# A graph-attention kernel: one node tile counted from ScalarE's steps, and T1 of head 0 summed on VectorE

## The chip, the core and the metric

The kernel runs on one core of a Trainium2 chip. The metric is the time of one execution on the device in microseconds (us), the median of a few runs. TensorE, VectorE (DVE), ScalarE (ACT), GpSimd (POOL) and SyncE (SP) each work through a queue of their own in order; semaphores connect them.

## What is computed

A two-layer graph attention network over 512 nodes with 768 features, a residual and a layer norm. There are 16,384 random edges, 8,192 in either direction, and 512 loops, 16,896 in all, sorted by destination. Per head of a layer:

```
h = x @ W                                    # 512 x 768
e = leaky_relu(h.a_s[src] + h.a_d[dst])
alpha = softmax of e over the edges of each dst
out[dst] = sum over its edges of alpha * h[src]   (+ b)
```

Layer 1 has 8 heads; its output (512 x 6144) goes through elu, and layer 2 has one head. The output is layernorm(x + layer 2).

## The kernel before

The edges enter only as counts. `cnt[dst, src]` says how many edges run from src to dst, and the softmax over edges becomes a dense softmax over 512 sources weighted by `cnt`; where there is no edge, `absent` holds a large number that pushes the exponent to zero. All matrix products of layer 1 are float32 and use a scheme with 7 products instead of 8 for each 2 x 2 block product (P1 to P7), so each head needs sums of blocks of its weights and of x: T1 = B11 + B12, T2 = T1 + B22, T3 = B12 + B22, T4 = T2 + B21 on the side of the weights, and `xS` with s1, s2, s4 (and s3 in place, in `xT`) on the side of x. P5 multiplies s1 by T1, P6 multiplies s2 by T2, P7 uses T3, P4 uses T4.

The start of the kernel, some 77 us, does three things at once. It loads x and the weights of heads 0 and 1. It counts the edges. And it projects head 0 (`first_projection`, 14 products) and the first four products of head 1. The order of all engines is written out by hand (`manual_schedule`).

**Counting.** The edges lie in 132 chunks of 128. For each chunk, `od` is a one-hot of the destination within a block of 32 nodes (the chunks are sorted, so a chunk touches one or two of the 16 blocks), and `os` is a one-hot of the source over 512 nodes. A matmul of `od` and `os` (L526) adds the chunk to 32 rows of a count in PSUM; four blocks of 32 rows make a node tile of 128, and four node tiles make the whole. 210 such matmuls are needed. `destinations` (L479) makes the `od` of a quarter of the chunks, `sources` the `os` of a batch of about 16 chunks: VectorE by one `is_equal` (L509), and from the third batch on a quarter of the chunks by ScalarE with two activations, |n - idx| and then relu(1 - that) (L502, L503). There are 32 `os` buffers. `count` sends the matmuls, and when a node tile is complete, `counted` copies it to `cnt` and makes `absent` (L393, L394). A program variable `flag` tells whether every edge fell within its chunk's blocks; if not, the whole is run again in a general way (it isn't here).

**The interleaving.** A loop over nine batches does, for each batch: the `od` of the quarters it needs, its `os`, some extra VectorE work (`extra`: the sums s1, s2, s4, s3, the logits of head 0), some products (`wants` says up to which one), and its counting matmuls. After the last products the logits are turned (`spread`, L434), lifted by ScalarE (L440), made leaky (L444) and ranked (L449) by VectorE. Then the remaining ten products of head 1 run beside the softmax of head 0.

**The weights of head 0.** W1[0] lies in `w0` (upper half) and `w1` (lower half); T1 lies in `w1t1`. SP loads `w0`'s and `w1`'s left halves, x, then the left half of the upper block into T1 (L150), then the right halves (L152), then the starts of T2 and T4 (L159). POOL then issues accumulating DMAs, each waiting for its operands, in this order: T1 += right half of the upper block (L378), T3 in place in `w0` (L379), T2 += T1 (L162), T4 += T2 (L163). The same loads and sums for head 1 follow on both queues (L105 to L117, L159 to L163).

Of the kernel before, what the change touches and what calls it, by code (L numbers as in the profile page):

```python
# [8 lines left out]
F32 = mybir.dt.float32  # L9
F16 = mybir.dt.float16  # L10
BF16 = mybir.dt.bfloat16
I32 = mybir.dt.int32
U16 = mybir.dt.uint16
AF = mybir.ActivationFunctionType
ALU = mybir.AluOpType
# [5 lines left out]
NO_EDGE = -1e30  # L21
# [15 lines left out]
def gat_pass(  # L37
# [16 lines left out]
    nc = tc.nc  # L54
# [66 lines left out]
    def load_w1(h, slot="w2"):  # L121
        return load_w(W1, h, slot, w1[:, h * D:(h + 1) * D])
# [15 lines left out]
    def block(m, r, cols):  # L138
        return m[r * HK * P:(r + 1) * HK * P, cols].rearrange("(k p) d -> p k d", p=P)
# [7 lines left out]
    b1_rows = ohp.tile([H * DC, P], F32, name="b1_rows")  # L147
    nc.sync.dma_start(b1_rows, b1.rearrange("(j p) -> j p", p=P))
    W1[0].append(wpool.tile([P, HK, HALF], F32, name="w1t1"))
    nc.sync.dma_start(W1[0][2], block(w1_0, 0, L))  # L150
    for r in (1, 0):
        nc.sync.dma_start(W1[0][r][:, :, R], block(w1_0, r, R))  # L152

    def sums_by_dma(W_, m, slot):

        lo_, hi_, t1_ = W_
        t2, t4 = (wpool.tile([P, HK, HALF], F32, name=f"{slot}t{j}") for j in (2, 4))
        for t_, cols in ((t2, R), (t4, L)):
            nc.sync.dma_start(t_, block(m, 1, cols))  # L159

        def additions():
            nc.gpsimd.dma_start(t2, t1_, accum_op=ALU.add)  # L162
            nc.gpsimd.dma_start(t4, t2, accum_op=ALU.add)  # L163
        return dict(P1=lo_[:, :, L], P2=hi_[:, :, L], P3=hi_[:, :, R], P4=t4, P5=t1_, P6=t2,
                    P7=lo_[:, :, R]), additions

# [152 lines left out]
    def logits(h, feats, t):  # L319
        for al, a, sign in zip(AL[h], A[h], (1.0, -1.0)):  # L320
            nc.vector.scalar_tensor_tensor(scr, feats[:, t, :], sign, a, op0=ALU.mult,
                                           op1=ALU.mult, accum_out=al[:, t:t + 1])
# [52 lines left out]
        ]  # L375
        return [pair(p, i, *rest) for p, *rest in steps for i in range(2)]

    nc.gpsimd.dma_start(W1[0][2], block(w1_0, 0, R), accum_op=ALU.add)  # L378
    nc.gpsimd.dma_start(W1[0][0][:, :, R], block(w1_0, 1, R), accum_op=ALU.add)  # L379
    additions0()  # L380

    load_w1(1, "w2")()
    B1, additions1 = sums_by_dma(W1[1], w1[:, D:2 * D], "w2")
    additions1()


    b1T = const.tile([P, H * DC], F32, name="b1T")
# [3 lines left out]
    def counted(t, ps):  # L391

        nc.scalar.copy(cnt[:, t, :], ps[:, :N])  # L393
        nc.scalar.activation(absent[:, t, :], ps[:, :N], AF.Relu, bias=far, scale=NO_EDGE)  # L394

    def first_projection(h, XA, B_):

# [64 lines left out]
    again = None  # L462
    if not general:

        order = []
        for g in range(NT):
            rs = [[c for c in range(EC) if int((c + 0.5) * P * N / E) // B == b] for b in range(g * 4, g * 4 + 4)]
            while any(rs):
                order.append([r.pop(0) for r in rs if r])
        hits = {}  # L470
        for b in (b for bs in blocks for b in bs):
            hits[b] = hits.get(b, 0) + 1
        todo = dict(hits)
        cps, done = {}, 0
        od = ohp.tile([P, NB, B], BF16, name="odw", bufs=1)

        def destinations(lo, hi):
            lo, hi = at[lo], at[hi]
            nc.vector.tensor_tensor(od[:, lo:hi, :],  # L479
                                    rel[:, lo:hi].unsqueeze(2).to_broadcast([P, hi - lo, B]),  # L480
                                    nodes[:, :B].unsqueeze(1).to_broadcast([P, hi - lo, B]),
                                    op=ALU.is_equal)

        def inside():
# [2 lines left out]
            nc.vector.tensor_scalar(below, rel, float(B), None, op0=ALU.is_lt)  # L487
            nc.vector.scalar_tensor_tensor(below, rel, 0.0, below, op0=ALU.is_ge, op1=ALU.mult, accum_out=found)


        nidx = ohp.tile([P, EC], F32, name="nidx")
        nc.scalar.activation(nidx, idx, AF.Copy, scale=-1.0)

        def sources(chunks, with_scalar, between):

            hot = {}
            shared = chunks[3::4] if with_scalar else []
            own = [c for c in chunks if c not in shared]
            for c in shared:
                hot[c] = ohp.tile([P, N], BF16, name="os", bufs=32)  # L500
                off = ohp.tile([P, N], F16, name="off", bufs=2)
                nc.scalar.activation(off, nodes, AF.Abs, bias=nidx[:, c:c + 1])  # L502
                nc.scalar.activation(hot[c], off, AF.Relu, bias=ones, scale=-1.0)  # L503
            for j, c in enumerate(own):
                if j == len(own) // 2:
                    for f in between:
                        f()
                hot[c] = ohp.tile([P, N], BF16, name="os", bufs=32)
                nc.vector.tensor_scalar(hot[c], nodes, idx[:, c:c + 1], None, op0=ALU.is_equal)  # L509
            return hot  # L510

        queues = [[] for _ in range(0, P, B)]

        def count(batch, hot, rest):


            nonlocal done
            for c, b in ((c, b) for wave in batch for c in wave for b in blocks[c]):
                queues[b * B % P // B].append((c, b, hot[c]))
            while any(queues) and (rest or all(queues) or sum(map(len, queues)) > 3):  # L520
                for c, b, h_ in [q_.pop(0) for q_ in queues if q_]:
                    t, r = b * B // P, b * B % P
                    if t not in cps:
                        pool, name = (bc, "bc") if t == 2 else (tr, "tr")
                        cps[t] = pool.tile([P, 512], F32, name=name)
                    nc.tensor.matmul(cps[t][r:r + B, :N], od[:, at[c] + b - blocks[c][0], :], h_,  # L526
                                     start=todo[b] == hits[b], stop=todo[b] == 1,
                                     tile_position=(0, r), skip_group_check=True)
                    todo[b] -= 1
            while done < NT and all(todo[b] == 0 for b in range(done * P // B, (done + 1) * P // B)):  # L530
                counted(done, cps[done])
                done += 1


        turns = {1: [(0, 1), (1, 1)], 3: [(2, 0), (3, 0), (2, 1), (3, 1)]}
        keep_warm(1)
        found = const.tile([P, 1], F32, name="found")
        pst = bc.tile([P, 512], F32, name="bc")
        wholes = len(items)

        s1, s2, s3, s4 = xsums
        extra = {0: [inside], 1: [s1, s2, s4], 3: [s3], 5: [lambda: logits(0, HS[0], 0)],
                 6: [lambda: logits(0, HS[0], 1), lambda: logits(0, HS[0], 2)], 7: [lambda: logits(0, HS[0], 3)]}
        wants = [3, 4, 7, 10, 12, 14, 16, 18]
        BW = 4
        batches = [order[i:i + BW] for i in range(0, len(order), BW)]
        pos, ready, quarter, waiting = 0, 0, EC // NT, []
        for n, batch in enumerate(batches):
            chunks = [c for wave in batch for c in wave]
            while ready <= max(chunks):  # L550
                destinations(ready, ready + quarter)
                ready += quarter
            if n == 3:
                nc.vector.tensor_scalar(flag, pst[:1, :1], -1.0, float(E), op0=ALU.mult, op1=ALU.add)
            hot = sources(chunks, n > 1, waiting)
            waiting = []
            for f in extra.pop(n, []):
                f()
            while n < len(wants) and pos < wants[n]:
                if pos == wholes:  # L560
                    pairs = projection(1, XA, B1)
                    items += [(m, e, False) for m, e in pairs[:4]]
                multiply, empty, on_vector = items[pos]
                multiply()
                if on_vector:
                    waiting.append(empty)
                else:
                    empty()
                pos += 1
                for t, r in turns.get(pos, []):  # L570
                    turn_x(t, r)
            if n == 2:
                turn_b1()
            if n + 1 == len(batches):
                spread(0)
                q = [lift(0, t) for t in range(NT)]
                for t in range(NT - 1):
                    leak(q[t])
                for t in range(NT - 1):
                    rank(q[t], t)  # L580
            if n == 1:
                nc.tensor.matmul(pst[:1, :1], found, ones, start=True, stop=True)
            if n == 4:
                again = nc.values_load(flag[:1, :1], min_val=0, max_val=E)
            count(batch, hot, n + 1 == len(batches))
        assert not extra and not waiting and pos == len(items) and done == NT
    else:
        for t in range(NT):
            ps = mm.tile([P, 512], F32, name="mm")
# [8 lines left out]
            for r in range(2):  # L598
                turn_x(t, r)
        turn_b1()  # L600
        for f in xsums:
            f()
        for m, e, _ in items:
# [441 lines left out]
```

## Time and profile before

| | us |
|---|---|
| median of 3 runs | 664.24 |
| lowest and highest | 663.87, 664.38 |
| the profiled execution | 663.6 |
| its span, first to last instruction | 661.8 |

| engine | busy us | share |
|---|---|---|
| TensorE matmuls | 645.7 | 98% |
| TensorE weight loads (beside them) | 400.1 | 60% |
| VectorE | 506.8 | 77% |
| ScalarE | 281.4 | 43% |
| GpSimd | 47.9 | 7% |

The profile describes one execution. "L306" is line 306 of the kernel; lines of the changed kernel differ. A row of a timeline gives the start, the length, the engine, the line, the operation with output<-input, shapes and a count, and in brackets how long the engine had been idle before and what released it. Waits are inferred from semaphore events, and some matmul records can be missing. TensorE has a granted clock, 1.00 for full and 0.50 for half; the profile lists it by stretches of time.

### The profile page before, as it was taken

To read this page: it belongs to the slowest core of one execution; us is meant where nothing else is said; L and a number is where in the kernel's file an instruction comes from. 1 tells how busy PE (TensorE), PEld (TensorE's weight loads), DVE (VectorE), ACT (ScalarE), POOL (GpSimd) and SP (SyncE) were. 2 spreads that over 40 slices of the span, in tenths; PEclk is the share of its full clock that TensorE was granted. 3 is DMA by queue.
4 is the path that set the end of the run, shared out by engine and by line. 5 is a ranking of instruction groups with operands and counts; after the bars stand their busy time and mean duration, and the time that the engine had idled before them with its cause. 6 is when DMAs were issued, how large, how long until landed. Compare 5 with 4: busy or idle time off the path is not lost.

```text
span 661.8 us, 7074 instructions
## 1 busy us (share of the span) xinstructions
PE 645.7 (98%) x2347; PEld 400.1 (60%) x2347; DVE 506.8 (77%) x1103; ACT 281.4 (43%) x477; POOL 47.9 (7%) x91
## 2 busy tenths in 40 slices
PE   9799899999999999999999999999999999999995
PEld 5354467555865577556855577556855545644553
DVE  7959689977778587777779587867676489866785
ACT  4289657260445216350635135440726033333440
POOL 3020011000100110010100110010000100000000
PEclk9799799999999999999999999999999999999998
DMA  9993179267902973077803892096605865000122
GB/s 321 289 272 89 35 241 279 76 167 164 269 14 49 265 209 90 14 222 162 215 0 75 239 241 58 17 255 195 146 1 146 217 213 132 24 1 0 30 59 76
DMA packets 74986, 92.06 MB, mean 139 GB/s; under 512 B 36742, under 2 KB 59326, under 8 KB 74942
## 3 DMA queue, kind: packets, MB, share of 16 engines
q1 hardware_dynamic: 60878, 69.31, 33.2%
q0 software_dynamic: 13376, 21.24, 18.6%
q10 hardware_dynamic: 688, 0.98, 0.5%
q8 instruction: 20, 0.33, 0.2%
q14 instruction: 24, 0.20, 0.1%
HBM read 79.20 MB, written 1.57 MB: 122 GB/s over the span
## 4 chain that ended last, share of the span: by engine, by line
PE 92%; DMA 4%; ACT 2%; issue 0%; DVE 0%; SPq 0%; ACTq 0%
PE mm L306 62%; PE mm L731 17%; PE mm L677 6%; DMA w1t<-in_L_gnn_W_dram 3%; PE mm L997 3%; PE held L306 2%; ACT off L502 1%; ACT os L503 1%; PE tr L526 1%; DMA hs<-in_x_dram 1%; PE bc L434 0%; PE tr L925 0%; PE tr L646 0%; PE bc L526 0%; ACT absent L394 0%
## 5 line engine op out<-in xcount | busy, mean ns | idle before, releaser
L306 PE MATMUL mm<-w,gT 128*128 128x384 f32 x288 | 97.4, 487 | 0.0
L306 PE MATMUL mm<-w,xT 128*128 128x384 f32 x264 | 88.2, 487 | 0.0
L306 PEld LDWEIGHTS mm<-w,gT 128*128 128x128 f32 x288 | 53.9, 190 | 35.7 <-issue 2.0
L306 PEld LDWEIGHTS mm<-w,xT 128*128 128x128 f32 x264 | 49.9, 190 | 35.5 <-issue 0.4
L451 ACT ACTIVATE q<-q,nmax 128x512 f32<-128x512 f32 x36 | 25.8, 721 | 89.9 <-DVE nmax L449 89.9
L306 PE MATMUL mm<-w1t,gS 128*128 128x384 f32 x180 | 60.7, 486 | 0.0
L306 PE MATMUL mm<-w2t,xS 128*128 128x384 f32 x168 | 58.2, 497 | 0.0
L735 ACT COPY u<-mm 128x256 f32<-128x256 f32 x18 | 6.7, 373 | 119.2 <-PE mm L731 119.2
L731 PE MATMUL mm<-PT,hs 128*128 128x256 f32 x216 | 52.6, 379 | 0.0
L364 DVE TENSOR_TENSOR h<-h,mm 128x384 f32<-128x384 f32 x72 | 39.6, 551 | 14.3 <-PE mm L306 13.8
L306 PEld LDWEIGHTS mm<-w1t,gS 128*128 128x128 f32 x180 | 34.1, 190 | 23.6
L306 PEld LDWEIGHTS mm<-w2t,xS 128*128 128x128 f32 x168 | 32.6, 195 | 23.6 <-issue 2.3
L731 PEld LDWEIGHTS mm<-PT,hs 128*128 128x128 f32 x216 | 41.0, 190 | 7.2 <-issue 0.4
L654 ACT COPY nr<-q 128x1024 uint16<-128x1024 uint16 x32 | 33.4, 1044 | 24.3 <-DVE q L640 17.5
L677 PE MATMUL mm<-PT,hs 128*128 128x512 f32 x96 | 41.6, 593 | 0.0
L659 ACT COPY PT<-zr 128x1024 uint16<-128x1024 uint16 x32 | 37.1, 1158 | 2.0 <-DMA zr<-nr 2.0
L731 PE MATMUL mm<-pS,gS 128*128 128x256 f32 x144 | 37.1, 380 | 0.0
L306 PE MATMUL mm<-w,gS 128*128 128x384 f32 x96 | 32.6, 486 | 0.0
L306 PE MATMUL mm<-w1t,gT 128*128 128x384 f32 x96 | 32.5, 487 | 0.0
L306 PE MATMUL mm<-w,xS 128*128 128x384 f32 x96 | 32.5, 487 | 0.0
L677 PEld LDWEIGHTS mm<-PT,hs 128*128 128x128 f32 x96 | 18.2, 190 | 22.9 <-issue 21.5
L106 POOL DMA_DIRECT2D w1t<-in_L_gnn_W_dram x7 | 9.0, 1279 | 316.7 <-PE mm L306 179.9
(183 smaller groups left out, 1079.8 us busy)
## 6 DMA issues: line engine op xcount, KB each, us to landing
w<-in_L_gnn_W_dram SPq DMA_DIRECT2D x90, 384.0 KB, 6.1
w<-in_L_gnn_W_dram POOLq DMA_DIRECT2D x16, 576.0 KB, 9.0
w1t<-in_L_gnn_W_dram SPq DMA_DIRECT2D x10, 576.0 KB, 4.5
w2t<-in_L_gnn_W_dram SPq DMA_DIRECT2D x10, 576.0 KB, 11.1
w1t<-in_L_gnn_W_dram POOLq DMA_DIRECT2D x8, 576.0 KB, 8.7
w2t<-in_L_gnn_W_dram POOLq DMA_DIRECT2D x8, 576.0 KB, 9.4
a_s<-in_L_gnn_a_src_dram SPq DMA_DIRECT2D x8, 384.0 KB, 5.1
a_d<-in_L_gnn_a_dst_dram SPq DMA_DIRECT2D x8, 384.0 KB, 5.4
```

What stands on the lines that cost most here:

```text
L106: nc.gpsimd.dma_start(t1, upper[:, :, R], accum_op=ALU.add)
L306: nc.tensor.matmul(ps[:, :HALF], A_[p][:, k, i * P:(i + 1) * P], B_[p][:, k, :], start=start and k == 0, stop=k == HK - 1, skip_group_chec ...
L364: nc.vector.tensor_tensor(a, a, ps, op=ALU.subtract if p == "P7" else ALU.add)
L451: nc.scalar.activation(q, q, AF.Exp, bias=nmax, scale=-1.0)
L502: nc.scalar.activation(off, nodes, AF.Abs, bias=nidx[:, c:c + 1])
L503: nc.scalar.activation(hot[c], off, AF.Relu, bias=ones, scale=-1.0)
L654: nc.scalar.copy(apart.rearrange("p (h n) -> p h n", h=2), q.bitcast(U16).rearrange("p (n h) -> p h n", h=2))
L659: nc.scalar.copy(PT.rearrange("p s n -> p (s n)").bitcast(U16).rearrange("p (s n h) -> p s n h", s=NT, h=2)[:, :, t * P:(t + 1) * P, :], p ...
L677: nc.tensor.matmul(ps[:, :N], HS[h][:, s, c * P:(c + 1) * P], PT[:, s, :], start=(s == 0), stop=(s == NT - 1))
L731: nc.tensor.matmul(bank[p][:, :HN], A_[p][:, k, c * P:(c + 1) * P], B_[p][:, k, :], start=over is None and k == 0, stop=k == 1, skip_group ...
L735: nc.scalar.copy(u, part("P1"))
L997: nc.tensor.matmul(ps[:, :cols.stop - cols.start], PT[:, s, t * P:(t + 1) * P], h2[:, s, cols], start=(s == 2), stop=(s == 1))
```

## The change

It has two parts, and what goes with them.

T1 of head 0 is no longer loaded and accumulated by DMA. VectorE adds the two halves of `w0` (128 x 1152 float32), and for that the right half of `w0` is loaded ahead of that of `w1`. The sums of the weights of both heads are now asked for inside the loop, in batch 1, in the order T1 (VectorE), T2, T3, T4.

The chunks of node tile S = 2 are taken out of the order of the others and spread over all batches. Their sources are made by ScalarE in one activation, as a step instead of a one-hot: sign(n + 0.5 - idx) is -1 below the source and 1 from it on. Half the difference of neighbouring columns of the summed steps is the count. `counted_by_steps` takes it from PSUM with a column put in front, VectorE takes the difference, and `absent` is made from that. All other chunks are VectorE's. A chunk that touches tile 2 and another tile is made in both forms. The steps of a batch are made a batch ahead, between the products. The sum for `flag` moves to another PSUM bank, and is made and read earlier.

```diff
     W1[0].append(wpool.tile([P, HK, HALF], F32, name="w1t1"))
-    nc.sync.dma_start(W1[0][2], block(w1_0, 0, L))
-    for r in (1, 0):
+    for r in (0, 1):
         nc.sync.dma_start(W1[0][r][:, :, R], block(w1_0, r, R))
...
-        def additions():
-            nc.gpsimd.dma_start(t2, t1_, accum_op=ALU.add)
-            nc.gpsimd.dma_start(t4, t2, accum_op=ALU.add)
+        additions = [lambda: nc.gpsimd.dma_start(t2, t1_, accum_op=ALU.add),
+                     lambda: nc.gpsimd.dma_start(t4, t2, accum_op=ALU.add)]
...
-    nc.gpsimd.dma_start(W1[0][2], block(w1_0, 0, R), accum_op=ALU.add)
-    nc.gpsimd.dma_start(W1[0][0][:, :, R], block(w1_0, 1, R), accum_op=ALU.add)
-    additions0()
-
-    load_w1(1, "w2")()
-    B1, additions1 = sums_by_dma(W1[1], w1[:, D:2 * D], "w2")
-    additions1()
+    def weight_sums():
+
+        nc.vector.tensor_tensor(W1[0][2], W1[0][0][:, :, L], W1[0][0][:, :, R], op=ALU.add)
+        additions0[0]()
+        nc.gpsimd.dma_start(W1[0][0][:, :, R], block(w1_0, 1, R), accum_op=ALU.add)
+        additions0[1]()
+        load_w1(1, "w2")()
+        B_, additions1 = sums_by_dma(W1[1], w1[:, D:2 * D], "w2")
+        for f in additions1:
+            f()
+        return B_
...
+    def counted_by_steps(t, ps):
+
+
+        steps = ohp.tile([P, N + 1], F32, name="steps")
+        nc.scalar.activation(steps[:, 1:], ps[:, :N], AF.Copy, scale=0.5)
+        nc.scalar.activation(steps[:, :1], ps[:, N - 1:N], AF.Copy, scale=-0.5)
+        nc.vector.tensor_tensor(cnt[:, t, :], steps[:, 1:], steps[:, :N], op=ALU.subtract)
+        nc.scalar.activation(absent[:, t, :], cnt[:, t, :], AF.Relu, bias=far, scale=NO_EDGE)
...
+        S = 2
+        order = {False: [], True: []}
...
-        nc.scalar.activation(nidx, idx, AF.Copy, scale=-1.0)
...
+        nc.scalar.activation(nidx, idx, AF.Copy, bias=0.5, scale=-1.0)
...
+        def one_hot(c, steps):
+            hot[c, steps] = o = ohp.tile([P, N], BF16, name="os", bufs=32)
+            if steps:
+                nc.scalar.activation(o, nodes, AF.Sign, bias=nidx[:, c:c + 1])
+            else:
+                nc.vector.tensor_scalar(o, nodes, idx[:, c:c + 1], None, op0=ALU.is_equal)
...
-        pst = bc.tile([P, 512], F32, name="bc")
...
-        extra = {0: [inside], 1: [s1, s2, s4], 3: [s3], 5: [lambda: logits(0, HS[0], 0)],
+        def ask():
+            nc.vector.tensor_scalar(flag, pst[:1, :1], -1.0, float(E), op0=ALU.mult, op1=ALU.add)
+
+        extra = {0: [inside], 1: [lambda: B1.update(weight_sums()), ask, s1, s2, s4], 3: [s3],
+                 5: [lambda: logits(0, HS[0], 0)],
...
-        BW = 4
-        batches = [order[i:i + BW] for i in range(0, len(order), BW)]
+        batches = []
+        for ours, theirs in ((16, 0), (8, 8), (8, 8), (12, 4), (12, 4), (12, 4), (13, 3), (14, 2), (4, 0)):
+            take = [order[k][:m] for k, m in ((False, ours), (True, theirs))]
+            del order[False][:ours], order[True][:theirs]
+            batches.append(take[0][:ours // 2] + take[1] + take[0][ours // 2:])
...
+            for k in sorted({c // quarter for c in batch} - made):
+                destinations(k * quarter, (k + 1) * quarter)
+                made.add(k)
+            sources(kinds(batch, False), waiting)
+            ahead = kinds(batches[n + 1], True) if n + 1 < len(batches) else []
+            items_here = max(wants[n] - pos if n < len(wants) else 0, 1)
+            share = -(-len(ahead) // items_here)
...
+                for c in ahead[:share]:
+                    one_hot(c, True)
+                del ahead[:share]
...
-            if n == 1:
+            if n == 0:
+                pst = mm.tile([P, 512], F32, name="mm")
                 nc.tensor.matmul(pst[:1, :1], found, ones, start=True, stop=True)
-            if n == 4:
+            if n == 3:
                 again = nc.values_load(flag[:1, :1], min_val=0, max_val=E)
```

More of the change, by code (lines that the diff above doesn't have):

```diff
@@ L463, in gat_pass @@
     if not general:
-        order = []
+        S = 2
+        order = {False: [], True: []}
         for g in range(NT):
@@ L468, in gat_pass @@
             while any(rs):
-                order.append([r.pop(0) for r in rs if r])
+                order[g == S] += [r.pop(0) for r in rs if r]
         hits = {}
@@ L473, in gat_pass @@
         todo = dict(hits)
-        cps, done = {}, 0
+        cps, done = {}, set()
         od = ohp.tile([P, NB, B], BF16, name="odw", bufs=1)
@@ L491, in gat_pass, with by_steps, kinds, sources @@
         nidx = ohp.tile([P, EC], F32, name="nidx")
-        nc.scalar.activation(nidx, idx, AF.Copy, scale=-1.0)
[L494 to L505, printed above, removed]
+        nc.scalar.activation(nidx, idx, AF.Copy, bias=0.5, scale=-1.0)
+        def by_steps(b):
+            return b * B // P == S
+        hot = {}
+        def one_hot(c, steps):
[4 more added lines that the diff above has]
+                nc.vector.tensor_scalar(o, nodes, idx[:, c:c + 1], None, op0=ALU.is_equal)
+        def kinds(batch, steps):
+            return [c for c in batch if any(by_steps(b) == steps for b in blocks[c])]
+        def sources(chunks, between):
+            for j, c in enumerate(chunks):
+                if j == len(chunks) // 2:
                     for f in between:
                         f()
-                hot[c] = ohp.tile([P, N], BF16, name="os", bufs=32)
-                nc.vector.tensor_scalar(hot[c], nodes, idx[:, c:c + 1], None, op0=ALU.is_equal)
-            return hot
+                one_hot(c, False)
         queues = [[] for _ in range(0, P, B)]
[L514 to L519, printed above, removed]
+        def count(batch, rest):
+            for c, b in ((c, b) for c in batch for b in blocks[c]):
+                queues[b * B % P // B].append((c, b, hot[c, by_steps(b)]))
             while any(queues) and (rest or all(queues) or sum(map(len, queues)) > 3):
@@ L523, in count @@
                     if t not in cps:
-                        pool, name = (bc, "bc") if t == 2 else (tr, "tr")
+                        pool, name = (bc, "bc") if t == S else (tr, "tr")
                         cps[t] = pool.tile([P, 512], F32, name=name)
@@ L529, in count @@
                     todo[b] -= 1
-            while done < NT and all(todo[b] == 0 for b in range(done * P // B, (done + 1) * P // B)):
-                counted(done, cps[done])
-                done += 1
+            for t in range(NT):
+                if t not in done and all(todo[b] == 0 for b in range(t * P // B, (t + 1) * P // B)):
+                    (counted_by_steps if t == S else counted)(t, cps[t])
+                    done.add(t)
         turns = {1: [(0, 1), (1, 1)], 3: [(2, 0), (3, 0), (2, 1), (3, 1)]}
@@ L537, in gat_pass @@
         found = const.tile([P, 1], F32, name="found")
-        pst = bc.tile([P, 512], F32, name="bc")
         wholes = len(items)
         s1, s2, s3, s4 = xsums
-        extra = {0: [inside], 1: [s1, s2, s4], 3: [s3], 5: [lambda: logits(0, HS[0], 0)],
+        def ask():
+            nc.vector.tensor_scalar(flag, pst[:1, :1], -1.0, float(E), op0=ALU.mult, op1=ALU.add)
+        extra = {0: [inside], 1: [lambda: B1.update(weight_sums()), ask, s1, s2, s4], 3: [s3],
+                 5: [lambda: logits(0, HS[0], 0)],
                  6: [lambda: logits(0, HS[0], 1), lambda: logits(0, HS[0], 2)], 7: [lambda: logits(0, HS[0], 3)]}
+        B1 = {}
         wants = [3, 4, 7, 10, 12, 14, 16, 18]
-        BW = 4
-        batches = [order[i:i + BW] for i in range(0, len(order), BW)]
-        pos, ready, quarter, waiting = 0, 0, EC // NT, []
-        for n, batch in enumerate(batches):
[L549 to L555, printed above, removed]
+        batches = []
[3 more added lines that the diff above has]
+            batches.append(take[0][:ours // 2] + take[1] + take[0][ours // 2:])
+        assert not any(order.values())
+        pos, made, quarter, waiting = 0, set(), EC // NT, []
+        for n, batch in enumerate(batches):
+            for k in sorted({c // quarter for c in batch} - made):
[5 more added lines that the diff above has]
+            share = -(-len(ahead) // items_here)
             waiting = []
@@ L571, in gat_pass @@
                     turn_x(t, r)
+                for c in ahead[:share]:
+                    one_hot(c, True)
+                del ahead[:share]
+            assert not ahead
             if n == 2:
@@ L580, in gat_pass @@
                     rank(q[t], t)
-            if n == 1:
+            if n == 0:
+                pst = mm.tile([P, 512], F32, name="mm")
                 nc.tensor.matmul(pst[:1, :1], found, ones, start=True, stop=True)
-            if n == 4:
+            if n == 3:
                 again = nc.values_load(flag[:1, :1], min_val=0, max_val=E)
-            count(batch, hot, n + 1 == len(batches))
-        assert not extra and not waiting and pos == len(items) and done == NT
+            count(batch, n + 1 == len(batches))
+        assert not extra and not waiting and pos == len(items) and len(done) == NT
     else:
@@ L600, in gat_pass @@
         turn_b1()
+        B1 = weight_sums()
         for f in xsums:
```

## The prediction

> **What bounds the kernel now.** I read the page first: TensorE is busy 98% of the span, so only its idle time and clock can be won. The row of granted clock says where.
>
> ```profile
> PE   9799899999999999999999999999999999999995
> PEclk9799799999999999999999999999999999999998
> ```
>
> Slices 2 and 5 (16.5 us each) are the soft ones; from slice 6 on nothing is lost until the tail. So the question is the first 77 us. The chain of waits in order of time names what ends there:
>
> ```profile
> 4.61 7.84 DMA w1t<-in_L_gnn_W_dram
> 12.45 0.30 issue
> 12.76 12.29 DMA w1t<-in_L_gnn_W_dram
> 25.04 0.14 issue
> 25.18 8.54 PE mm L306 x18
> ...
> 69.60 0.73 ACT os L503
> 70.33 0.04 issue
> 70.37 1.01 PE tr L526 x3
> 71.38 18.90 PE mm L306 x53
> ```
>
> Two holes: T1 arrives by two DMAs in a row (a load, then an accumulate) at 25.04, and before 71.3 TensorE waits for ScalarE's one-hot rows. TensorE's timeline prices both:
>
> ```profile
> 25.18 6.61 PE L306 MATMUL mm<-w1t,xS 128*128 128x384 f32 x12 [4.35 <-DMA w1t<-in_L_gnn_W_dram]
> 33.84 1.70 PE L526 MATMUL tr<-os,odw 128*32 128x512 bf16 x27
> 42.66 4.14 PE L306 MATMUL held<-w,xT 128*128 128x384 f32 x12
> 67.64 0.97 PE L526 MATMUL tr<-os,odw 128*32 128x512 bf16 x8 [1.88 <-ACT os L503]
> 71.31 5.75 PE L306 MATMUL mm<-w2t,xS 128*128 128x384 f32 x12
> 84.64 4.03 PE L306 MATMUL mm<-w2t,xS 128*128 128x384 f32 x12
> ```
>
> The bracket is the idle time and its releaser. A pair of products takes 4.07 from start to start (42.66 to the next row at 46.73), but 6.44 after the first hole (25.18 to 31.62) and 5.59 after the second (71.31 to 76.90): each hole also costs clock. Half-microsecond windows show it; the granted clock is the third number from the right:
>
> ```profile
> 23.00:23.50 0.50, 0.00 (x0) 0.00 (x0) 0.50 (x1) 0.00 (x0) 0.00 (x0) 0.89 1.11 264
> 30.00:30.50 0.50, 0.50 (x2) 0.30 (x2) 0.50 (x2) 0.00 (x0) 0.00 (x0) 0.79 1.22 280
> 67.50:68.00 0.50, 0.36 (x8) 0.19 (x8) 0.00 (x0) 0.50 (x2) 0.00 (x0) 0.76 0.10 37
> 74.50:75.00 0.50, 0.50 (x3) 0.23 (x2) 0.50 (x3) 0.50 (x2) 0.00 (x0) 0.91 0.00 0
> ```
>
> It falls to half at 23.4 and returns at 30.2; falls at 67.6 and returns at 74.5.
>
> **T1.** Removed: one 576 KB load on SP and one 576 KB accumulate on POOL. The right half of w0 now takes the load's place in SP's queue, so I give it that landing, 12.45; the other loads move up one place. Added: one VectorE addition, 128x1152 f32, 1.35 (the same shape in the later heads' T2 row). Its place in VectorE's queue decides. From 14.14 (end of the `below` pair) I lay out the new order with the old durations: destinations 1.87, five one-hots at 0.263 each 1.31, a `hs` addition 0.46, five one-hots 1.31: 19.1. T1 to 20.45, the flag to 20.55, s1 0.9: 21.5. The operands have been there for 6.6 us, so the wait that T1 adds costs nothing; without that cover it holds the flag, s1, s2, s4 and every later one-hot.
>
> TensorE before P5: ScalarE now puts Sign rows ahead of the four x evacuations, which start at 14.9 instead of 14.39; the transposes that wait for them, and the 22 + 24 counting matmuls and P2, end near 21.3 instead of 20.83. So P5 starts at 21.6, not 25.18: 3.6 less. With a gap of 0.3 instead of 4.35 the clock stays up: P5's pair takes 4.07, not 6.44: 2.4 less. P3 starts at 25.65 instead of 31.62.
>
> POOL's queue: T2's accumulate moves ahead of T3's, and T4, and both accumulates of head 1, follow. T2 waits for T1 (20.5). The SBUF-to-SBUF accumulate took 5.5 without traffic (head 1) and 8.7 with; the worst in the trace is 12.3 (T1's own). I take 8.7, since SP still loads: T2 lands at 29.2, P6 wants it at 31.6: hidden, slack 2.4; at 12.3 it is late by 1.2. T3 (14.0 in the trace) is issued near 21.4, lands by 35.4, and P7 wants it at 37.3. T4 (8.3 from T2's landing) lands near 37.5 to 41; P4 wants it at 42.4. Hidden.
>
> **Counting by steps.** ScalarE had 48 one-hot activations (24 chunks, Abs then Relu, 1.37 a chunk). Now it has 39 single Sign activations (33 chunks of tile 2 and six that touch it). The trace has no Sign: the nearest row is the 128x512 Abs, 0.62 to its successor where that does not depend on it, 0.74 where it does. I take 0.63, as nothing depends on it: 39 x 0.63 = 24.6 instead of 32.9. ScalarE, saturated from 36.4 to 72.6, gets 8.3 us of air, and none of its rows are needed by the last count. VectorE: 104 one-hots instead of 108 (-1.05), T1 (+1.35), the difference of steps (128x512 f32, 0.68): +1.0 in all. It had 7.6 us of waits between 32.9 and 46.8, which this comes out of.
>
> TensorE from 25.65 has the old work with 13 more counting matmuls ahead of the turn of the logits (156 instead of 143; 27 took 1.62, so 0.06 each, +0.8). Products in pairs at 4.07, counts at 0.06: P6 at 31.6, P7 at 37.3, P4 at 42.4, head 1's P1 at 48.4, its P2 at 54.1, the last big count from 58.2 to 59.6 (64.78 before: 5.2 earlier). VectorE against that: after P6's additions at 36.3 it has 13 + 6 + 13 + 15 one-hots, destinations, two additions and four pairs of logits, 22.9, without a wait: each batch is 1 to 3 us ahead of its count, logits ready at 59.1. TensorE remains the bound, just.
>
> The end. At 59.6 tile 2 is complete. ScalarE copies its steps (0.59 like `cnt`) and one column (not in the trace; 0.1 to 0.25, the 128x48 `nb1T` took 0.23; I take 0.2): 60.5. VectorE waits for that, subtracts (61.15), and only then makes the last four one-hots (62.2). Queued behind its wait: those four, so 8 counting matmuls and P6 of head 1. P6 starts at 62.45 instead of 71.31: from 59.6 that is 2.85 where it was 6.53, 3.7 less. `absent` of tile 2 now waits for VectorE, and the four lifts behind it on ScalarE; they start at 61.85, and `leak` 0.4 later relative to P6 than before.
>
> [...] The row: the clock fell at 67.6 after only 1.88 us without a matmul, 1.5 us of work still lying within the last 3.4 us. [...] The new gap is 1.35 (60.05 to 61.4) plus a sparse microsecond. [...] This gap being shorter than the row's, I take no loss, and keep 3.4 for the range.
>
> After P6 the softmax of head 0 runs beside five pairs. Before, PT was complete at 91.92 and TensorE asked for it at 92.38, the sum t2 ending at 93.37 just for its use at 93.42. TensorE now comes 1.7 sooner, the softmax 0.4 later, and VectorE's waits for TensorE in between (0.45 and 1.38) go. That leaves t2 late by about 0.3 (bounds 0 and 1.5).
>
> Moved at no cost: the count of found edges goes to an mm bank and its flag to before s1 (0.1 us of VectorE, in the 0.3 gap's cover); reading the flag comes one batch earlier, when it is 14 us old; without that cover it would stop every queue.
>
> **Sum against the profiled execution:** -3.6 - 2.4 + 0.8 - 3.7 - 1.7 + 0.3 = -10.3 on 663.6 (span 661.8 and 1.8 around it), 653.3. The median shown, 664.24, is 0.64 above that execution, so 653.9.
>
> **Rivals.**
> 1. Clock or accumulate late (chance 0.22). [...] For: the fall at 67.6. Against: 8.7 is the contended row.
> 2. VectorE becomes the bound (0.12). It is only about 1 us ahead at the end; if its waits for TensorE stay (the 32 one-hot buffers, now partly held by Sign rows made a batch ahead), the old 7.6 us of waits come back: old end 66.9 plus 1.0, the wait for the steps 1.4, and 0.3: P6 at 69.6, clock kept: 664.24 - 1.7 - 1.7, near 661; half of it 657.5.
> 3. Slower (0.04). T1 is in order on VectorE. If the right half of w0 lands late, everything behind waits. From T1's start VectorE has 40 us of work to P6, so P6 starts at landing + 40. Against the old 71.3 with the clock saving of 1.7, it decides from a landing of 33: at 36 it gives 667. Against: this place in the queue landed at 12.45.
> 4. The steps do not relieve the end, as the last count waits for something else (0.02): only T1's part stays, 6 us: 658.
>
> **Numbers.** The forecast has 0.60, 652.5 to 655; 650.5 would need the gap at 60 closed as well. The range 651 to 658.5 takes in rivals 1 and 4 and half of 2. 0.2% is 1.3 us, about what a measurement of this kernel tells from no change. Faster 0.94, same 0.02, slower 0.04.
>
> **What would show it.** T1 row of 1.35 near 19 to 20.5 with no DMA wait before it; P5 near 21.6 in 4.1; clock 1.00 from 23 to 31; T2 landing before P6 asks; no ScalarE wait in counting; a gap of about 1.3 at 60; head 1's P6 near 62.5. A DMA named before P6 or P7, VectorE named before the counts, or a clock of 0.5 beyond 60 would prove the steps above wrong.

## The result, and the profile after

The changed kernel takes 653.81 us (653.58 to 653.86, 6 runs) against 664.31 in the same session (662.44 to 664.79, 6 runs): a ratio of 0.9845, 95% interval 0.9832 to 0.9858. In a second session it took 653.80 against 663.11, a ratio of 0.9859 (0.9843 to 0.9875). The forecast was 653.9. The profiled execution spans 651.8 us instead of 661.8.

The page's rows of TensorE and of its granted clock, in 40 slices of the span:

```profile
PE   8999999999999999999999999999999999999995
PEclk9999999999999999999999999999999999999998
```

The two soft slices are gone from both rows. TensorE's timeline shows where each hole went (start, length, work, and in brackets the idle time before it and its releaser):

```profile
21.74 4.14 PE L304 MATMUL mm<-w1t,xS 128*128 128x384 f32 x12
25.71 2.10 PE L304 MATMUL mm<-w,xS 128*128 128x384 f32 x6
...
42.81 4.14 PE L304 MATMUL held<-w1t,xT 128*128 128x384 f32 x12 [0.30 <-DVE hs L427]
...
60.10 0.65 PE L445 MATMUL tr<-ident,al_s 128*128 128x128 f32 x4
61.49 1.39 PE L542 MATMUL tr<-os,odw 128*32 128x512 bf16 x8 [0.74 <-DVE os L516]
62.81 4.14 PE L304 MATMUL mm<-w2t,xS 128*128 128x384 f32 x12
66.79 4.03 PE L304 MATMUL mm<-w,xT 128*128 128x384 f32 x12
```

P5 starts at 21.74 without a bracket, and its pair reaches P3 at 25.71, 3.97 later. No ScalarE releaser stands before a count any more. One hole of more than 0.6 us is left, after the turn of the logits at 60.10. The chain of waits names its links:

```profile
59.79 0.60 ACT steps L402
60.39 0.07 ACT steps L403
60.46 0.02 issue
60.48 0.69 DVE cnt L404
61.17 1.06 DVE os L516 x4
62.23 0.04 issue
62.28 0.61 PE tr L542 x3
```

That is the new wait: ScalarE copies the steps, VectorE takes their difference and only then makes the last four one-hots. The clock in this hole (third number from the right) stays at 1.00:

```profile
60.50:61.00 0.50, 0.25 (x3) 0.10 (x2) 0.50 (x1) 0.00 (x0) 0.00 (x0) 1.00 0.94 332
61.00:61.50 0.50, 0.01 (x3) 0.01 (x2) 0.50 (x3) 0.29 (x1) 0.00 (x0) 1.00 0.72 215
62.00:62.50 0.50, 0.37 (x4) 0.11 (x2) 0.22 (x1) 0.50 (x2) 0.00 (x0) 1.00 0.86 320
```

On the side of the sums of weights, the timelines of VectorE and of POOL:

```profile
18.66 1.35 DVE L378 TENSOR_TENSOR w1t<-w 128x1152 f32<-128x1152 f32 x1
...
20.33 1.03 POOL L160 DMA_DIRECT2D w1t<-w1t  x1 [16.75 <-DVE flag L560]
21.05 1.62 POOL L380 DMA_DIRECT2D w<-in_L_gnn_W_dram  x1
29.64 1.25 POOL L161 DMA_DIRECT2D w1t<-w1t  x1 [6.97 <-DMA w1t<-w1t]
```

T1 has no bracket: it waits for nothing that the trace shows. (The releaser `flag` of POOL's row is T1's neighbour on VectorE; T1 itself ended at 20.0.) T2 has landed at 29.64, when T4 is released, and P6 starts at 31.59.

### The profile page after: what moved, and what is told of

It is laid out like the page before. It is cut to its first block, busy times and chain, and to the rows that moved or that the text cites. A ratio compares the mean times of both kernels' runs of the same rounds, so it can differ in the third digit from the quotient of the medians.

```text
span 651.8 us, 7058 instructions
## 1 busy us (share of the span) xinstructions
PE 640.2 (98%) x2347; PEld 397.6 (61%) x2347; DVE 507.4 (78%) x1102; ACT 273.8 (42%) x469; POOL 47.0 (7%) x90
## 4 chain that ended last, share of the span: by engine, by line
PE 97%; ACT 1%; DVE 1%; issue 0%; DVEq 0%
PE mm L304 64%; PE mm L763 17%; PE mm L709 6%; PE mm L1029 3%; PE held L304 2%; PE tr L542 1%; PE bc L177 1%; ACT os L514 1%; PE bc L445 0%; PE bc L542 0%; PE tr L957 0%; PE tr L678 0%; ACT xT L205 0%; PE mm L204 0%; DVE os L516 0%
## 5 line engine op out<-in xcount | busy, mean ns | idle before, releaser
L304 PE MATMUL mm<-w2t,xS 128*128 128x384 f32 x168 | 56.6, 487 | 0.0
```

The costliest lines, as they stand in the source:

```text
L304: nc.tensor.matmul(ps[:, :HALF], A_[p][:, k, i * P:(i + 1) * P], B_[p][:, k, :], start=start and k == 0, stop=k == HK - 1, skip_group_chec ...
```

## The experiments

All are timed against the kernel before in the same session; the median of that moved between 663.1 and 663.7 from session to session.

### The two parts alone

T1's part put into the kernel before:

```diff
-    nc.sync.dma_start(W1[0][2], block(w1_0, 0, L))
-    for r in (1, 0):
+    for r in (0, 1):
...
-    nc.gpsimd.dma_start(W1[0][2], block(w1_0, 0, R), accum_op=ALU.add)
+        nc.vector.tensor_tensor(W1[0][2], W1[0][0][:, :, L], W1[0][0][:, :, R], op=ALU.add)
...
+        extra = {0: [inside], 1: [lambda: B1.update(weight_sums()), s1, s2, s4], 3: [s3], 5: [lambda: logits(0, HS[0], 0)],
...
```

> The kernel before with T1's part alone (VectorE adds the halves of w0, w0's right half loaded first; counting as before). Theory (two separate holes, each with its clock): P5 starts near 21.5 instead of 25.2, a pair of products takes 4.1 instead of 6.4 there, and ScalarE's one-hots, which follow the products, come 5.9 sooner too; the hole at the end stays with its half clock. 5.9 us less than before: 658.4 beside 664.3. Rival (ScalarE is the bound of the whole stretch, T1's hole is covered by it): the end stays where it was, within 1.5 us of before. Rival (VectorE, 1.35 us fuller, becomes the bound): 661 or so, with VectorE named before the counts.

Measured: 656.98 against 663.58, 6.6 less; ratio 0.9905 (0.9887 to 0.9924). TensorE's timeline:

```profile
21.13 4.14 PE L304 MATMUL mm<-w1t,xS 128*128 128x384 f32 x12
...
61.12 1.04 PE L528 MATMUL tr<-os,odw 128*32 128x512 bf16 x8 [1.88 <-ACT os L505]
62.49 1.05 PE L528 MATMUL tr<-os,odw 128*32 128x512 bf16 x7 [0.32 <-ACT os L505]
63.86 1.01 PE L528 MATMUL tr<-os,odw 128*32 128x512 bf16 x3 [0.32 <-ACT os L505]
64.80 5.65 PE L304 MATMUL mm<-w2t,xS 128*128 128x384 f32 x12
```

The first hole is gone. The second came along, nearly the same (1.88, 0.32, 0.32 with ScalarE as releaser; before 1.88, 0.40, 0.32), 6.5 us sooner and with its slow pair (64.80 to 70.28). So ScalarE's backlog was a length behind the products, not a fixed end, and both rivals fall: VectorE, 1.35 fuller, stood idle for 4.08 us around this hole, as it did in the kernel before (4.05).

The counting's part alone, the loads and accumulates of the kernel before put back into the changed one:

```diff
-    for r in (0, 1):
+    nc.sync.dma_start(W1[0][2], block(w1_0, 0, L))
+    for r in (1, 0):
...
-        nc.vector.tensor_tensor(W1[0][2], W1[0][0][:, :, L], W1[0][0][:, :, R], op=ALU.add)
+    nc.gpsimd.dma_start(W1[0][2], block(w1_0, 0, R), accum_op=ALU.add)
...
```

> The changed kernel with T1 by two DMAs as before; counting by steps stays. Theory (two separate holes): P5 at 25.2 with half clock as before; no ScalarE wait at the end, the last hole near 1.3 us and the clock kept there: head 1's P6 near 68.8 instead of 71.3, 1.7 us of clock, in all 4 us less than before, 660.2. So the two parts add up to the whole 10. Rival (the parts need each other): less than 2 us of gain, with the rest only when T1 comes early. Rival (the steps alone make the gain): near 654.

Measured: 658.74 (657.02 to 660.29) against 663.58, 4.8 less; ratio 0.9922 (0.9903 to 0.9940). The profiled execution is the slowest of the six, 660.29:

```profile
25.52 6.78 PE L305 MATMUL mm<-w1t,xS 128*128 128x384 f32 x12 [4.11 <-DMA w1t<-in_L_gnn_W_dram]
...
69.24 4.14 PE L305 MATMUL mm<-w2t,xS 128*128 128x384 f32 x12
73.21 4.03 PE L305 MATMUL mm<-w,xT 128*128 128x384 f32 x12
```

Head 1's P6 starts at 69.24, 2.07 sooner than before, and its pair takes 3.97 instead of 5.59: 3.7 together, near the 4 that was expected. The first hole is there as before. The other five runs took 657.02 to 659.08, less than expected, and the mean clock goes with the time: 0.993 at 660.29, 0.995 in three, 0.997 in the two fastest. So the clock is the likely cause of the spread of 3 us; that it was lost at this hole is not shown, as only one of the six has a trace. The parts, 6.6 and 4.8, add up to 11.4 where the whole is 10.5 (9.3 in the second session): within that spread, as two separate holes would.

### What a hole costs in clock

Zeros multiplied in the two holes of the kernel before, their result used by nothing:

```diff
+            if n == 2:
+                warm = mm.tile([P, 512], F32, name="mm")
+                for _ in range(9):
+                    nc.tensor.matmul(warm, zeros[:, :P], zeros, start=True, stop=True)
...
+            if n + 1 == len(batches):
+                warm = mm.tile([P, 512], F32, name="mm")
+                for _ in range(4):
+                    nc.tensor.matmul(warm, zeros[:, :P], zeros, start=True, stop=True)
```

> The kernel before with 9 idle-time matmuls of zeros in TensorE's first hole and 4 in the hole near 66; they compute nothing that is used. Theory (each hole costs its clock besides its length): clock 1.00 throughout, the pair after the first hole takes 4.1 instead of 6.4 and the one before head 1's second pair 3.9 to 4.1 instead of 5.6: 4.1 us less than before, and less spread between runs. Rival (the half clock is not on the path, as ScalarE's one-hots set the end anyway): only the second hole's 1.7 or less.

Measured: 660.79 against 663.11, 2.3 less; ratio 0.9967 (0.9954 to 0.9980); one run of six at 659.28, five between 660.64 and 661.45. The matmuls had been sized by those at the kernel's start (9 in 4.02); here 9 took 2.12, and in the one execution with a trace (659.28; clock 1.00 in the half-microsecond windows from 15.0 to 62.5, the pairs behind the two holes 3.94 and 3.97) 2.07 and 1.02 us of the holes stayed open. So the number was doubled to 18 and 8:

> The kernel before with 18 and 8 matmuls of zeros in its two holes instead of 9 and 4 (one took 0.22 us there, so they fill 4 and 1.8 us). Theory (each hole costs its clock, in the runs before only some executions were spared): clock 1.00 in every execution, 659.3 as in the one spared execution of the smaller fill, 4 us less than before. Rival (filling changes nothing more): 660.8 with the same spread.

Measured: 659.10 against 663.69; ratio 0.9945 (0.9930 to 0.9960). Four runs lie between 659.01 and 659.11 (mean clock 0.996 to 0.998), two at 660.57 and 660.67 (0.994). The trace is of one of the four:

```profile
25.27 4.11 PE L306 MATMUL mm<-w1t,xS 128*128 128x384 f32 x12
...
68.48 4.14 PE L306 MATMUL mm<-w2t,xS 128*128 128x384 f32 x12
```

P5 starts no sooner than before (25.27, 25.18), so nothing of the first hole's length is saved, and the 4.6 us by which the four runs are shorter are clock: the two pairs (2.5 and 1.6), and 0.4 in the last counts before P6, which took 0.59 instead of 1.01. Clock 1.00 in every execution had been expected, and two of the six missed it. Two gaps of 0.75 us between ScalarE's last rows are still open in the trace; whether the clock fell there in those two runs is not known.

In the row of before the clock fell with 1.88 us without a matmul; that a shorter hole costs no clock was the author's estimate. The hole that the change leaves was made longer by computing the difference three times over, and then seven times:

```diff
-        nc.vector.tensor_tensor(cnt[:, t, :], steps[:, 1:], steps[:, :N], op=ALU.subtract)
+        for _ in range(3):
+            nc.vector.tensor_tensor(cnt[:, t, :], steps[:, 1:], steps[:, :N], op=ALU.subtract)
```

> The changed kernel with the difference of the steps computed three times over instead of once (same values), 1.2 us more of VectorE in the hole at 60, so TensorE stands idle for about 2.0 us there in one piece and 3.5 us in all. [...] By the row of before (it fell after 1.88 us without a matmul): the clock falls to 0.50 near 62 to 65, 1.5 to 3.4 us more on top, 656.5 to 658.4.

Measured: 655.08, 655.26, 656.21, 656.40 and 656.50; ratio of the median 0.9885 (0.9866 to 0.9903). TensorE's timeline and the half-microsecond windows of the profiled execution, 656.50:

```profile
62.99 1.82 PE L543 MATMUL tr<-os,odw 128*32 128x512 bf16 x8 [2.19 <-DVE os L517]
64.74 5.05 PE L304 MATMUL mm<-w2t,xS 128*128 128x384 f32 x12
```

```profile
63.00:63.50 0.50, 0.50 (x5) 0.21 (x5) 0.50 (x3) 0.50 (x2) 0.00 (x0) 0.71 0.54 178
66.50:67.00 0.50, 0.50 (x2) 0.21 (x2) 0.50 (x3) 0.43 (x1) 0.00 (x0) 0.88 0.00 0
```

The clock fell at 63.2, after 2.19 us without a matmul, and came back at 66.6. By their mean clock two runs (0.997) were spared and three (0.994 to 0.995) were not, and 1.2 us lie between the groups, less than the 1.5 to 3.4 of the expectation, which were the author's estimate. So a hole of 2.19 us was enough in some executions, as 1.88 had been in the row of before. Why the same program is hit in one execution and spared in the next these runs do not show.

The same hole with 5 matmuls of zeros in it, to see whether the upper group goes with it:

> The run with the difference computed three times over, with 5 matmuls of zeros (used by nothing) put into its hole on TensorE. [...]

Measured: 655.11 (654.78 to 655.23, 4 runs), mean clock 0.996 to 0.998. The upper group is gone, so its 1.2 us were the clock.

Seven times over, by an estimate 4.2 us more of VectorE in the hole (six more differences of 0.70 each, as the run's chain of waits has them):

> [...] Theory: the clock falls in every execution, and the time is 4.2 us and 1.7 to 3.4 us of clock more than the changed kernel: 659.7 to 661.4, with less spread than with the 2.2 us hole. Rival (the clock has no part): 658.0.

Measured: 659.62 (659.54 to 660.43, 5 runs), mean clock 0.992 to 0.994 in all five; ratio 0.9946 (0.9932 to 0.9961).

```profile
65.68 1.89 PE L543 MATMUL tr<-os,odw 128*32 128x512 bf16 x8 [5.09 <-DVE os L517]
67.50 5.58 PE L304 MATMUL mm<-w2t,xS 128*128 128x384 f32 x12
```

The pair behind this hole takes 5.42 (67.50 to 72.92) where it takes 3.98 in the changed kernel. Going by the mean clock of each run, three sizes of this hole stand beside each other now: 0.74 tripped the clock in none of ten runs, 2.19 in three of five, 5.09 in five of five. In these runs the length in one piece does not decide alone: with T1's part alone the 1.88, followed by two gaps of 0.32, tripped it in five of five (0.992 to 0.995), while with the counting's part alone, where the trace has a hole of 4.11, two of six runs stayed at 0.997.

### How late T1 may be

The right half of w0 loaded behind the other blocks of head 0:

```diff
-    for r in (0, 1):
-        nc.sync.dma_start(W1[0][r][:, :, R], block(w1_0, r, R))
+    nc.sync.dma_start(W1[0][1][:, :, R], block(w1_0, 1, R))
...
     load_a(0, a_src1[0], a_dst1[0])
+    nc.sync.dma_start(W1[0][0][:, :, R], block(w1_0, 0, R))
```

> The changed kernel with the right half of w0 loaded behind w1's, T2's and T4's blocks and both logit vectors, 2.5 MB later in SP's queue: at the 0.37 MB a microsecond of the traces it lands near 19.3, so that T1 begins there instead of at 18.7. Theory (T1's wait is covered by 6 us, and P5 waits for TensorE's own counting): P5 within 0.2 of 21.7; 653.8 to 654.1. Rival (any delay of T1 moves all that is queued behind it on VectorE): 0.6 to 0.7 us more, 654.5.

Measured: 654.42 (654.29 to 655.06) against 653.80 for the changed kernel in another session, 0.6 more; ratio to before 0.9865 (0.9848 to 0.9881). The VectorE and TensorE timelines of the profiled execution (655.06):

```profile
20.70 1.36 DVE L378 TENSOR_TENSOR w1t<-w 128x1152 f32<-128x1152 f32 x1 [1.85 <-DMA w<-in_L_gnn_W_dram]
...
23.04 4.14 PE L304 MATMUL mm<-w1t,xS 128*128 128x384 f32 x12 [1.00 <-DVE xS L284]
```

T1 came 2.04 later, P5 1.30 later, and the span grew by 1.2. The difference, 0.74, is what TensorE's own counting had covered. The landing was mis-sized (20.6, not 19.3), so the expected start of T1 is missed, and the outcome decides for neither theory as put: the first 0.7 is free, what comes on top is paid.

Later still, behind seven more loads:

```diff
     def weight_sums():
 
+        rest1 = load_w1(1, "w2")
+        nc.sync.dma_start(W1[0][0][:, :, R], block(w1_0, 0, R))
         nc.vector.tensor_tensor(W1[0][2], W1[0][0][:, :, L], W1[0][0][:, :, R], op=ALU.add)
...
```

> The same, but the right half of w0 loaded behind head 1's upper block and six rows of its weights too; it lands near 27, and T1 ends near 28.4. Prediction's sum for a late landing (VectorE has 40 us of work from T1 to head 1's P6): P6 near 67, 4 us more than the changed kernel, 658. Rival (TensorE sets the pace from P5 on, and its hole costs the clock as well): P5 at 29.5 with half clock, head 1's P6 near 71.5, 9 us more, 662.6, so that the change would be slower than before from a landing of about 28 already.

Measured: 667.85 (667.35 to 668.18) against 663.69; ratio 1.0069 (1.0053 to 1.0086), slower than before.

```profile
31.38 1.36 DVE L379 TENSOR_TENSOR w1t<-w 128x1152 f32<-128x1152 f32 x1 [12.36 <-DMA w<-in_L_gnn_W_dram]
...
33.71 5.59 PE L303 MATMUL mm<-w1t,xS 128*128 128x384 f32 x12 [12.02 <-DVE xS L283]
```

The load landed at 31.3, not near 27. T1 starts 12.7 later than in the changed kernel and P5 12.0, again 0.7 less, and the time is 14.0 more: the hole and its clock (the pair takes 5.43). From T1's start to head 1's P6, at 76.24, it is 45 us, not 40 as VectorE's sum had it. TensorE sets the pace: from P5 to P6 it is 42.53, against 41.07 in the changed kernel, and the 1.46 between them are the slow pair. This run is 4.2 slower than before, so by an estimate from it the change would have lost its gain from a landing of about 27.

### A version that beats both

First the difference moved behind the last one-hots, and `absent` of tile 2 behind the four lifts:

```diff
...
-        nc.vector.tensor_tensor(cnt[:, t, :], steps[:, 1:], steps[:, :N], op=ALU.subtract)
-        nc.scalar.activation(absent[:, t, :], cnt[:, t, :], AF.Relu, bias=far, scale=NO_EDGE)
+        later.extend([difference, missing])
...
                 spread(0)
+                later[0]()
                 q = [lift(0, t) for t in range(NT)]
+                later[1]()
```

> The changed kernel with VectorE's difference of the steps put behind the last four one-hots, and absent of tile 2 behind the four lifts. Theory (the hole at 60 is VectorE's wait for the steps and the difference, with the last one-hots queued behind): the four one-hots end near 61.2 instead of 62.2, head 1's P6 starts near 61.8 instead of 62.8; 0.9 to 1.0 us less than the changed kernel: 652.9. Rival (the softmax of head 0 sets when the aggregation starts, so what P6 gains is given back there): 653.8, unchanged, with a wait before the aggregation.

Measured: 652.48 (652.30 to 652.75); ratio to before 0.9836 (0.9818 to 0.9853). Head 1's P6 starts at 61.84 instead of 62.81, and nothing of that is given back: the last pair ahead of the aggregation starts at 77.42 instead of 78.40.

Then three more edits with it: 40 one-hot buffers, the last four one-hots made by ScalarE, and ScalarE's steps of batch 1 mostly behind the evacuations of x:

```diff
-            hot[c, steps] = o = ohp.tile([P, N], BF16, name="os", bufs=32)
+            hot[c, steps] = o = ohp.tile([P, N], BF16, name="os", bufs=40)
...
-            sources(kinds(batch, False), waiting)
+            sources([] if n + 1 == len(batches) else kinds(batch, False), waiting)
+            last = kinds(batches[-1], False) if n == 6 else last
...
+                some = 0 if n == 0 and pos == 2 else len(ahead) if n == 0 and pos == 3 else share
...
+                if (n, pos) in ((6, wants[6]), (7, wants[6] + 1)):
+                    for c in last[:2]:
+                        by_scalar(c)
```

> The changed kernel with the difference of the steps behind (as in the run before), the four one-hots of the last batch made by ScalarE with Abs and Relu in its idle time at 52 to 59, ScalarE's Sign rows of batch 1 behind the x evacuations except three, and 40 one-hot buffers instead of 32. Theory (what is left before 62 is VectorE, full from 42 on, and two waits of 0.3 to 0.7): last count ready with the logits, head 1's P6 near 60.5 instead of 62.8; 651.3. Rival (ScalarE's added 5.4 us delays the steps, and the lifts behind them): 652 to 653, no better than moving the difference alone.

Measured: 651.81 (651.48 to 652.25) beside 653.80 for the changed kernel in the same session, 2.0 less; ratio to before 0.9829 (0.9815 to 0.9843). The chain of waits between 36 and 64 now names only TensorE; its end:

```profile
54.22 4.07 PE mm L304 x12
58.28 0.75 PE tr L558 x10
...
59.69 0.58 PE tr L452 x4
60.27 0.97 PE tr L558 x8
61.25 2.78 PE mm L304 x8
```

P6 is at 61.18, not at the expected 60.5. P5 starts at 21.64, only 0.1 sooner than in the changed kernel, though TensorE's counts before it end 0.3 sooner: VectorE began T1 at 19.31 (18.66 there), and P5 waits for s1, which ends at 21.59. So T1 on VectorE is now what holds P5. From P5 to P6 no row of TensorE has a bracket.

## Why the prediction was right, step by step

The sum had six terms, read here from the two timelines:

| term | predicted | measured | from |
|---|---|---|---|
| P5 starts sooner | -3.6 | -3.44 | 25.18 to 21.74 |
| clock of its pair | -2.4 | -2.47 | 6.44 to 3.97 |
| P3 to the turn of the logits | +0.8 | +1.23 | 33.16 to 34.39 |
| the turn to head 1's P6 | -3.7 | -3.82 | 6.53 to 2.71 |
| clock of P6's pair | -1.7 | -1.61 | 5.59 to 3.98 |
| sum t2 late | +0.3 | 0 | 15.48 from the second pair to the aggregation in both |
| sum | -10.3 | -10.1 | span 661.8 to 651.8 |

- **The mechanism** is what the runs with one part alone show: two holes, each with a length and a clock, that come off one by one. The zeros show the clock's share separately.
- **The number** is closer than the working. The terms are each within 0.45, but errors of +0.43 and -0.3 offset each other. The profiled execution was forecast at 653.3 and took 653.82; the 0.64 added for the median of before made up for that. The mechanism earned the range; the hit within 0.1 is luck.
- **T1 without a wait** held, at 18.66 instead of 19.1. The cover of 6.6 us that the prediction named is that of the operands before T1; when they landed here the trace does not show. The cover that counts, between s1 and P5, is 0.74.
- **POOL's queue** held: T2 landed at 29.64, forecast 29.2.
- **Sign** cost what the Abs row had said: ten in a row took 6.23, 0.62 each.
- **The term that was mis-sized** is the middle. The prediction had VectorE run "without a wait" from 36.3. It waited 0.73 at 41.7 for a one-hot buffer that a counting matmul still held, and TensorE 0.30 for VectorE at 42.8:

```profile
41.67 0.62 DVE L516 TENSOR_SCALAR os<-nodes,idx 128x512 bf16<-128x512 f16 x2 [0.73 <-PE tr L542]
42.21 1.01 DVE L427 TENSOR_TENSOR hs<-hs,held 128x384 f32<-128x384 f32 x2
```

  The lost time lies here: P4 starts 5.63 behind P7, where the forecast had 5.1, and the stretches on either side are within 0.2 of it. VectorE also made 105 one-hots, not 104. The 32 buffers were named in the second rival, but with the whole 7.6 us of old waits. In the last version, with 40 buffers and two more edits, both waits are gone; the buffers alone were not tried.
- **t2** was not late: VectorE's waits for TensorE behind P6 went from 0.45 and 1.38 to 0.21, as much as the pair had shrunk.
- **The clock in the hole at 60** was not lost, as the sum had taken it. The gap had been put at 1.35, and it was 0.74. No run shows that a hole of 1.35 costs no clock, on which the -1.7 for P6's pair stands: it was the author's estimate, and the runs showed a hole of 0.74, the clock at 1.00 in it and 1.61 less for the pair. At 2.19 the clock was lost in three of five. The 3.4 us of loss kept for the range is an estimate as well, half of the 6.83 us at half clock behind the row of before; the fall in the hole of 2.19 cost 1.2.
- **The slower rival** had the right mechanism and a wrong price: landing + 40 came from VectorE's work, and landing + 45 was measured. It decides from about 27, by the estimate above, not from 33.

## What to carry to other kernels

The two holes of the kernel before had two prices each, their length (4.35 and 1.88 us without a matmul) and the slow clock after them (2.47 and 1.61 on the pair behind); read both, and see whether a part of the gain comes from the clock alone. When a step moves from a DMA to an in-order engine, what matters is not how long its operands have been there but how much the next consumer has still to do: here it was 0.74 us. After the bound is relieved, look at what is queued behind each new wait: here four one-hots stood behind a difference that nobody needed yet.

## What the runs showed of the hardware

TensorE's clock fell to half in some executions and not in others of one program, with a hole of 2.19 us: by their mean clock three of five (0.994 to 0.995) against two (0.997), 656.4 against 655.2 on the mean of each group. One of the three, 656.50, has a trace, and its clock is 0.50 from 63.2 to 66.6. The kernel before has levels of its own, as the mean clock of each run of the experiments' three sessions shows: 661.9 to 662.7 at 0.992, 662.6 to 663.1 at 0.990, 663.5 to 665.0 at 0.987. Whether they have the same reason is not shown, as only one execution of it has a trace.

The traces also show how long the clock stayed down. Worked out from half-microsecond windows, six stretches at half lasted 3.41 us (the hole of 2.19), 6.82 or 6.83 (both of the kernel before, and one in each run with one part alone) and 10.24 (the latest load of w0): one, two or three times 3.41. In the kernel before the falls, at 23.39 and 67.76 (the prediction had read 67.6), lie 44.37 apart, 13 times 3.41 to within 0.04; one trace does not tell this from chance. In the 3.41 us ahead of each of the six falls TensorE was busy for 0.00 to 1.6 us.

Nine matmuls of zeros of 512 columns in bfloat16 took 4.02 us at the kernel's start, where the profile also shows a clock of 1.00, and 2.12 in the first hole of the kernel before.
